# Writing the instruction order of a scan stage and an attention stage by hand on four engines, with side work handed out in small steps

## Chip, cores and metric

The kernel runs on one core of one Trainium2 chip. The metric is the time of one execution in microseconds of device time. Before the change it is 973.29 us, the median of 3 runs (973.04, 973.29, 975.01).

A core has five engines that run side by side, each with its own queue of instructions: PE (TensorE: matrix products and transposes), DVE (VectorE), ACT (ScalarE), POOL (GpSimd) and SP (SyncE, which here only issues transfers). A queue is worked off in order, and an instruction whose input isn't there holds all that stand behind it on its engine. Products land in PSUM, everything else lives in SBUF; DRAM is reached by DMA.

## The reference, cut to what is computed

Four sequences of 512 rows and 128 columns pass through one layer, all in f32:

```python
x = x + A(layernorm(x))        # rmsnorm, selective scan, then mixture of experts
x = x + F(layernorm(x))        # feed-forward, weights are integers / 127
x = x + B(layernorm(x))        # latent attention, 16 heads, causal
x = x + F(layernorm(x))
...
# the scan inside A, 256 channels by 16 states, over 512 rows
h = dA * h + (d_t * x_t)[..., None] * B_t[:, None, :]
y = jnp.einsum('ben,bn->be', h, C_t)
...
# experts inside A: 8 experts, the 2 best of each row
ye = silu(hs @ Wg[e]) * (hs @ Wu[e]) @ Wd[e]
out = out + w_e[:, None] * ye
```

## The kernel before, in words

**Layout.** One sequence is four tiles of 128 rows. `b` counts sequences (0 to 3), `t` row tiles, `e` halves of the 256 channels. Two groups of two sequences share an expert pass: group 0 is sequences 0 and 1, group 1 is 2 and 3.

**Scan stage** (L446 to L758). `front(b)` (L519 to L603) prepares a sequence: normalized rows `hn` and `h0`, transposed (`pt`), convolution products `pm` (L538), `xi`, `sz`, the products for `bc` and `delta`, and `du` (L603, POOL). Then 16 states are scanned one by one, 64 steps in all (`scan(s)`, L635). A step has one chain: PE spreads a row over the partitions (`pb`, L621), DVE multiplies (`bx`, L646), DVE scans (`hst`, L650), POOL multiplies with the row of C (`hc`, L655), PE sums over the states (`yp`, L631). ACT makes the decays of the step two ahead (`da`, L611). `close(b)` (L664) turns `yp` into the output of the scan and the input of the experts, routes every row to two experts (`route`) and gives it a place in a list sorted by expert (`number`). `scatter(b)` writes the rows to the sorted list in DRAM (L268, POOL, 32 indirect transfers in all).

**Experts.** `plan(g)` turns the counts of a group into 23 tiles of 128 rows. `experts(g)` works through them: SP loads the rows `xt` and the weights `wgu` and `wd` (0.83 MB a tile); PE transposes (`mpt`, L353), multiplies (`mpg` and `mpu`, L362, 8 products), ACT takes tanh (L367), DVE two products (`halved`, L323 and L324), PE multiplies (`mpd`, L373), ACT copies (`ym`, L377), SP stores. `combine(b)` gathers the two results of each row (L387, POOL) and adds them (L391, DVE).

**Attention stage** (L761 to the end). `ffn` is a layer norm, a transpose, three pairs of products (`pg` L783, `pu` L785) with tanh and `halved`, and the products `fpd` (L792). `project(b)` makes the latent queries and keys, splits each value into three bf16 parts and stores them in DRAM (`q_d`, `k_d`); `fill(u)` loads them back, stacked, for a unit `u` of 8 heads (8 units). `maxima(u)` finds each row's largest score (`sc`, L886 and L890 on PE, 22 reductions `mx`, L895, on DVE) and sends it through DRAM (`m_d`) into the stack. `exps(G)` makes scores and exponentials of 4 heads (`st` L937 and L945 on PE, `p` L950 on ACT), `weigh(G)` the weighted sums (`po`, L960), `divide(G)` the quotients. 16 of these `G` are run, with `maxima` of the next unit and a queue `work` of side streams between them. Each stream is a Python generator: a `yield` ends one step, and `work.step()` traces the next step of the first stream in the queue.

**What sets the order.** The generators fix only the order in which the program is traced. The order in which each engine gets its instructions is chosen by a scheduler, which goes through what is ready by a priority and an estimated duration; it may put instructions of a side stream before or behind those of the main loop. After the scan stage everything that is left of the queue is emptied (L758), then come `first_ffn(0)`, `project(0)`, the loads of units 0 and 1, and the queue `first_ffn(1), project(1), experts(1), combine(2), first_ffn(2), project(2), combine(3), first_ffn(3)`, 12 steps of it beside `maxima(0)`.

At the start all four sequences are loaded on SP, all their row statistics are taken together in one chain of small DVE instructions on 16 columns (L485 to L496), integer weights are converted (L507) and the two sorted lists are filled with zeros (two transfers of 4 MB, L514).

Of the kernel before, what the change touches and what calls it, by code (L numbers as in the profile page):

```python
# [16 lines left out]
P = 128  # L17
# [9 lines left out]
NG = 4  # L27
EPS = 1e-5
WBUFS = 3
PBUFS = 12  # L30
GROUPS = [[0, 1], [2, 3]]
BIG = 3.0e38


@with_exitstack
def block_kernel(ctx, tc, x, rms1_w, rms2_w, in_proj_w, conv_w, conv_b, x_proj_w,
# [8 lines left out]
    xs = []  # L45
    for b in range(B):
        xt = keep.tile([P, NT, C], F32, tag="x", name=f"x{b}")
        nc.sync.dma_start(xt, x[b].rearrange("(t p) c -> p t c", p=P))
        xs.append(xt)
# [8 lines left out]

    r1w = load("r1w", [P, 1, 1], column(rms1_w, 1), nc.scalar)
    w_in = load("w_in", [P, 2 * EI], in_proj_w, nc.scalar)  # L60
# [4 lines left out]
    A = load("A", [P, NE, NS], A_log.rearrange("(c p) n -> p c n", p=P), nc.scalar)  # L65
    Dk = load("Dk", [P, NE, 1], column(D_skip, NE), nc.scalar)
    w_op = load("w_op", [P, NE, C], out_proj_w.rearrange("(c p) m -> p c m", p=P))
    r2w = load("r2w", [P, 1, 1], column(rms2_w, 1))
    w_rt = load("w_rt", [P, NEXP], router_w)
    w_qk = const.tile([P, 2 * KVL], F32, tag="w_qk", name="w_qk")  # L70
    nc.sync.dma_start(w_qk[:, 0:KVL], W_dqT)
    nc.sync.dma_start(w_qk[:, KVL : 2 * KVL], W_dkvT)
    w_dq = load("w_dq", [KVL, C], W_dq)
    w_uq = load("w_uq", [KVL, C], W_uqT)
    w_uk = load("w_uk", [P, KVL], W_uk)
    w_uv = load("w_uv", [P, KVL], W_uv)
    w_o = load("w_o", [P, C], W_oT)
# [64 lines left out]
    def rsqrt(v, n, pool=small, tag="rs"):  # L142

        r = pool.tile([P, n], F32, tag=f"{tag}{n}", name="rs_r")
        t = pool.tile([P, n], F32, tag=f"{tag}t{n}", name="rs_t")
        nc.vector.tensor_scalar(
            t.bitcast(I32), v.bitcast(I32), 1, None, ALU.logical_shift_right
        )
        nc.vector.tensor_scalar(
            r.bitcast(I32), t.bitcast(I32), -1.0, float(0x5F3759DF), ALU.mult, ALU.add  # L150
        )
        for _ in range(3):
            nc.vector.tensor_tensor(t, r, r, ALU.mult)
            nc.vector.scalar_tensor_tensor(t, t, -0.5, v, ALU.mult, ALU.mult)
            nc.vector.scalar_tensor_tensor(r, t, 1.5, r, ALU.add, ALU.mult)
        return r
# [11 lines left out]
    def layernorm(dst, src):  # L168
        mv = moments(src)
        v = small.tile([P, NT], F32, tag="v", name="ln_v")  # L170
        nc.vector.tensor_scalar(v, mv[:, :, 1], EPS, None, ALU.add)
        r = rsqrt(v, NT)
        for t in range(NT):
            nc.vector.tensor_scalar(
                dst[:, t, :], src[:, t, :], mv[:, t, 0:1], r[:, t : t + 1], ALU.subtract, ALU.mult
            )

# [9 lines left out]
    def transposed(ps, dst, src, scale=None):  # L187

        pt = ps.tile([P, L], F32, tag="mm", name="pt")
# [7 lines left out]
    hs = [keep.tile([P, NT, C], F32, tag="hs", name=f"hs{b}") for b in range(B)]  # L197
# [18 lines left out]
    ps = ctx.enter_context(tc.tile_pool(name="ps_m", bufs=1, space=PSUM))  # L216
# [9 lines left out]
    def number(b):  # L226
# [12 lines left out]
        nc.vector.tensor_copy(tot, pr[:, 1].rearrange("p j e -> p e j"))  # L239
# [14 lines left out]
        nc.vector.tensor_tensor(row, inc.rearrange("p e j -> p j e"), pr[:, 0], ALU.add)  # L254
# [71 lines left out]
    def experts(g):  # L326
# [4 lines left out]
        xT, wgu, wd, hidden = {}, {}, {}, {}  # L331
        for i in range(NTILES + 2):
            if i < NTILES:
                e = nc.sync.value_load(both[0:1, 0, i : i + 1], min_val=0, max_val=NEXP - 1)
                at = nc.sync.value_load(
                    both[0:1, 1, i : i + 1], min_val=0, max_val=NEXP * ROWS - P
                )
                xt = wt.tile([P, C], F32, tag="xt", name="xt", bufs=3)
                nc.sync.dma_start(xt, sorted_x[g][bass.ds(at, P), :])
# [3 lines left out]
                wd[i] = wt.tile([P, NFC, C], F32, tag="wd", name="wd", bufs=WBUFS)  # L343
# [3 lines left out]
            if i >= 2:  # L347
                th, pg, pu = hidden.pop(i - 2)
                hT = wt.tile([P, NFC, P], F32, tag="mh", name="mh")
                halved(hT, th, pg, pu)  # L350
            if i < NTILES:
                pt = ps.tile([P, P], F32, tag="mm", name="mpt")
                nc.tensor.transpose(pt, xt, ident)  # L353
                xT[i] = wt.tile([P, P], F32, tag="xTm", name="xTm", bufs=3)
                nc.scalar.activation(xT[i], pt, AF.Copy, scale=r2w[:, 0, :])  # L355
            if 1 <= i <= NTILES:
                x, w = xT.pop(i - 1), wgu.pop(i - 1)
                pgu = []
                for k in range(2):
                    pp = ps_s.tile([P, NFC, P], F32, tag="sc", name=("mpg", "mpu")[k])  # L360
                    for f in range(NFC):
                        nc.tensor.matmul(  # L362
                            pp[:, f, :], w[:, k, f * P : (f + 1) * P], x, start=True, stop=True
                        )
                    pgu.append(pp)
                th = wt.tile([P, NFC, P], F32, tag="thm", name="thm")
                nc.scalar.activation(th, pgu[0], AF.Tanh, scale=0.5)  # L367
                hidden[i - 1] = th, *pgu
            if i >= 2:
# [6 lines left out]
                y = wt.tile([P, C], F32, tag="ym", name="ym")  # L376
                nc.scalar.copy(y, pd)  # L377
                nc.sync.dma_start(sorted_y[g][(i - 2) * P : (i - 1) * P, :], y)
            yield

    def combine(b):

        g = place[b][0]
        for t in range(NT):
            for k in range(2):
# [4 lines left out]
                )  # L390
                nc.vector.scalar_tensor_tensor(  # L391
                    base[b][:, t, :], yk, gates[b][:, t, k : k + 1], base[b][:, t, :],
                    ALU.mult, ALU.add,
                )
                yield

    class Queue:
# [20 lines left out]
    by_head = w_up.rearrange("p (d h) -> p h d", h=NH)  # L418
    nc.vector.tensor_copy(by_head[0:KVL], w_uq.rearrange("p (h d) -> p h d", d=HS))
    pk = ps.tile([P, L], F32, tag="mm", name="pk")  # L420
    nc.tensor.matmul(pk[:, 0:C], w_uq, w_dq, start=True, stop=True)
    m1 = const.tile([P, C], F32, tag="m1", name="m1")
    nc.vector.tensor_copy(m1, pk[:, 0:C])
    pk = ps.tile([P, L], F32, tag="mm", name="pk")
    nc.tensor.matmul(pk[KVL:P, 0:C], w_uk, m1, start=True, stop=True)
    nc.vector.tensor_copy(
        by_head[KVL:P], pk[KVL:P, 0:C].rearrange("p (h d) -> p h d", d=HS)
    )
    pk = ps.tile([P, L], F32, tag="mm", name="pk")
    nc.tensor.matmul(pk[KVL:P, 0:C], w_uv, w_o, start=True, stop=True)  # L430
    veff = const.tile([P, C], F32, tag="veff", name="veff")
    nc.vector.tensor_copy(veff[KVL:P, :], pk[KVL:P, 0:C])

    vs = []
    for i in range(2):


        va = const.tile([P, NT, NH * (HS + 1) + 32], F32, tag=f"va{i}", name=f"va{i}")
        nc.gpsimd.memset(va, 1.0)
        vs.append(va)  # L440


    nc.scalar.activation(A, A, AF.Exp)
    nc.vector.tensor_scalar(A, A, -1.0, None, ALU.mult)
    work = Queue()
    with ExitStack() as first:  # L446
# [11 lines left out]
        cwb = w3.tile([P, EI, KW], F32, tag="hst", name="cwb", bufs=2)  # L458
        nc.scalar.dma_start(cwb, conv_w.rearrange("e o k -> o e k").to_broadcast([P, EI, KW]))
        for k in range(KW):  # L460
            nc.vector.tensor_tensor(w_k[:, k, :], w_in[:, 0:EI], cwb[:, :, k], ALU.mult)


        w_bc = w1.tile([P, NE, 3, 2 * NS], F32, tag="w_bc", name="w_bc")
        nc.vector.tensor_copy(
            w_bc, w_xp[:, :, DTR:].unsqueeze(2).to_broadcast([P, NE, 3, 2 * NS])
        )
        pick32 = w1.tile([96, 2 * NS], F32, tag="pick32", name="pick32")
        nc.vector.tensor_reduce(
            pick32, ident[0:96, 0:96].rearrange("p (g c) -> p c g", g=3), AX.X, ALU.add  # L470
        )
        pick = w1.tile([96, 2 * NS], BF16, tag="pick", name="pick")
        nc.vector.tensor_copy(pick, pick32)
# [12 lines left out]
        for b in range(B):  # L486
            moments(xs[b], mv0[:, b])
        v = w1.tile([P, B * NT], F32, tag="v0", name="v0")
        var = mv0.rearrange("p b t s -> p (b t) s")[:, :, 1]
        nc.vector.tensor_scalar(v, var, EPS, None, ALU.add)  # L490
        r0 = rsqrt(v, B * NT, w1, "ln")
        nc.vector.tensor_tensor(v, r0, r0, ALU.mult)
        nc.vector.tensor_tensor(v, v, var, ALU.mult)
        nc.vector.tensor_scalar(v, v, EPS, None, ALU.add)
        r01 = rsqrt(v, B * NT, w1, "rms")
        nc.vector.tensor_tensor(r01, r01, r0, ALU.mult)  # L496


        def integers(tag, srcs, dsts):
            raw = w1.tile([P, NE, L], F32, tag=tag, name="raw").bitcast(I32)  # L500
            raw = raw.rearrange("p e l -> p (e l)")
            for i, (src, dst) in enumerate(zip(srcs, dsts)):
                part = raw[:, i * HID : (i + 1) * HID]
                if len(dst.shape) == 3:
                    part = part.rearrange("p (c m) -> p c m", c=NHC)
                nc.sync.dma_start(part, src)
                nc.vector.tensor_scalar(dst, part, 1.0 / 127.0, None, ALU.mult)  # L507

        integers("sp_y", (w_gateT, w_upT), (fwg, fwu))
# [616 lines left out]
```

## Time and profile before

| what | before |
|---|---|
| median of 3 runs | 973.29 us |
| profiled execution: time | 975.5 us |
| profiled execution: span | 973.8 us |
| granted TensorE clock, mean | 0.853 |
| PE busy | 747.4 us (77%), 3588 products |
| DVE busy | 625.7 us (64%), 1266 instructions |
| ACT busy, POOL busy | 332.7 us, 272.7 us |
| moved by DMA | 92.69 MB, mean 95 GB/s |

The profile shows one execution. Its time is 2.2 us over the median, and the 1.7 us between time and span lie outside what the engines do. A line of a group reads: line of the kernel, engine, operation, tile written and tiles read, shapes, count; then the time busy and the mean of one in ns; then the engine's idle time ahead of the group and what ended it. "Idle" is only a loss where the engine sets the pace. A row of the table of windows reads: the window, its length, then busy time and count for PE, its weight loads, DVE, ACT and POOL, then the granted PE clock, the share of time that the DMA engines were busy, and GB/s.

### The profile page before, as it was taken

The numbers are of one execution on the slowest core, as the hardware profiler recorded it, in microseconds if no ns is written. First come the engines' busy times: TensorE is split into PE (matmuls) and PEld (weight loads), VectorE is DVE, ScalarE is ACT, GpSimd is POOL, SyncE is SP. The second block draws the span as 40 slices with busy tenths as digits, with TensorE's granted clock in tenths as the row PEclk, the third lists the DMA queues.
The fourth block names the chain that finished last, engine by engine and source line by source line (L and its number), as shares of the span: only waits on it lengthen the run. The fifth ranks groups of instructions, "written<-read, shape, count | busy, mean of one in ns | idle before, by whom it ended". The sixth has DMA issues, their size and how long they took to land.

```text
span 973.8 us, 11231 instructions
## 1 busy us (share of the span) xinstructions
PE 747.4 (77%) x3588; PEld 407.9 (42%) x3588; DVE 625.7 (64%) x1266; ACT 332.7 (34%) x576; POOL 272.7 (28%) x190
## 2 busy tenths in 40 slices
PE   0878567766687976787266899979478999999894
PEld 0322222323234743575123366866333445444342
DVE  6279899789988899744754655542257475655523
ACT  0477322352236422321011044324311454433440
POOL 2046664476456443613620000000320010000000
PEclk9989796887699988989577589989776899989898
DMA  8612121111115752563146063855400342100000
GB/s 255 235 48 73 43 65 54 44 44 54 55 48 173 218 159 81 156 205 103 44 122 162 18 166 88 242 176 158 112 20 30 87 116 63 39 13 14 3 11 11
DMA packets 81084, 92.69 MB, mean 95 GB/s; under 512 B 9441, under 2 KB 56489, under 8 KB 79849
## 3 DMA queue, kind: packets, MB, share of 16 engines
q1 hardware_dynamic: 77105, 86.81, 30.2%
q0 software_dynamic: 2048, 4.20, 1.5%
q10 hardware_dynamic: 1872, 0.97, 0.4%
q8 instruction: 28, 0.46, 0.2%
q14 instruction: 31, 0.25, 0.1%
HBM read 70.71 MB, written 21.17 MB: 94 GB/s over the span
## 4 chain that ended last, share of the span: by engine, by line
PE 46%; DVE 27%; issue 11%; DMA 7%; ACT 5%; POOL 2%; SPq 1%; ACTq 0%; POOLq 0%; DVEq 0%
DVE hst L650 9%; PE po L960 6%; DVE bx L646 5%; PE yp L631 4%; PE sc L886 4%; PE st L937 4%; PE mpd L373 3%; PE pg L783 3%; DMA xt<-xg 3%; PE mpu L362 3%; PE mpg L362 2%; DVE mx L895 2%; PE fpd L792 2%; DMA yk<-yg,rows_y 2%; PE pm L538 2%
## 5 line engine op out<-in xcount | busy, mean ns | idle before, releaser
L631 PE MATMUL yp<-hc,ident 128*128 128x512 f32 x256 | 165.9, 755 | 69.0 <-POOL hc L655 66.8
L655 POOL TENSOR_TENSOR hc<-hst,cs 128x1024 f32<-128x1024 f32 x64 | 151.2, 2362 | 159.3 <-DVE hst L650 31.4
L650 DVE TENSOR_TENSOR_SCAN hst<-da,bx 128x1024 f32<-128x1024 f32 x64 | 145.9, 2280 | 2.8
L895 DVE TENSOR_REDUCE mx<-sc 128x1 f32<-128x512 f32 (+3 forms) x176 | 109.1, 638 | 43.0 <-PE sc L890 40.8
L611 ACT ACTIVATE da<-delta,A 128x512 f32<-128x512 f32 (+1 forms) x128 | 86.0, 713 | 141.4 <-DVE hst L650 103.1
L950 ACT ACTIVATE p<-st 128x512 f32<-128x512 f32 x160 | 90.9, 597 | 102.7 <-PE st L945 101.3
L631 PEld LDWEIGHTS yp<-hc,ident 128*128 128x128 f32 x256 | 53.6, 229 | 145.3 <-POOL hc L655 109.7
L646 DVE TENSOR_TENSOR bx<-du,pb 128x1024 f32<-128x1024 f32 x64 | 78.5, 1226 | 28.3 <-PE pb L621 24.0
L886 PE MATMUL sc<-ks,qs 72*128 72x128 bf16 (+3 forms) x256 | 71.4, 339 | 9.4 <-DVE mx L895 7.9
L960 PE MATMUL po<-p,va 128*32 128x512 f32 (+3 forms) x512 | 76.3, 447 | 0.0
L323 DVE SCALAR_TENSOR_TENSOR thm<-thm,mpg 128x512 f32<-128x512 f32 x46 | 31.4, 684 | 67.4 <-ACT thm L367 67.4
L387 POOL DMA_INDIRECT yk<-yg,rows_y x32 | 30.4, 950 | 138.5 <-DMA ks<-k_d 128.1
L937 PE MATMUL st<-qs,ks 75*128 75x512 bf16 (+3 forms) x256 | 63.8, 313 | 1.3 <-ACT p L950 0.9
L373 PE MATMUL mpd<-wd,mh 128*128 128x128 f32 x368 | 55.0, 296 | 2.7 <-ACT xTm L355 1.9
L362 PE MATMUL mpu<-xTm,wgu 128*128 128x128 f32 x368 | 53.6, 288 | 3.6 <-DVE mh L324 1.9
L373 PEld LDWEIGHTS mpd<-wd,mh 128*128 128x128 f32 x368 | 49.4, 206 | 13.9 <-ACT xTm L355 9.4
L986 POOL TENSOR_TENSOR base<-x,yn 128x512 f32<-128x512 f32 x4 | 5.1, 1267 | 177.4 <-DVE yn L981 177.4
L362 PE MATMUL mpg<-xTm,wgu 128*128 128x128 f32 x368 | 54.1, 290 | 0.6 <-DVE thm L323 0.6
L362 PEld LDWEIGHTS mpg<-xTm,wgu 128*128 128x128 f32 x368 | 50.4, 207 | 4.1 <-DVE thm L323 1.7
L362 PEld LDWEIGHTS mpu<-xTm,wgu 128*128 128x128 f32 x368 | 48.9, 204 | 7.3 <-DVE mh L324 4.5
L890 PE MATMUL sc<-maskq,identb 128*128 128x128 bf16 (+2 forms) x176 | 48.1, 273 | 0.0
L886 PEld LDWEIGHTS <-qs 72*128 72x128 bf16 x256 | 25.6, 109 | 42.0 <-issue 35.4
(229 smaller groups left out, 1079.9 us busy)
## 6 DMA issues: line engine op xcount, KB each, us to landing
cs<-c_d SPq DMA_DIRECT2D x64, 256.0 KB
wgu<-in_Wg_dram SPq DMA_DIRECT2D x46, 256.0 KB
wgu<-in_Wu_dram SPq DMA_DIRECT2D x46, 256.0 KB
wd<-in_Wd_dram SPq DMA_DIRECT2D x46, 256.0 KB
xg<-zero SPq DMA_DIRECT2D x2, 4096.0 KB
k_d<-parts SPq DMA_DIRECT2D x12, 384.0 KB
qs<-q_d SPq DMA_DIRECT2D x24, 192.0 KB
ks<-k_d SPq DMA_DIRECT2D x24, 192.0 KB
```

Of the source, the lines that this page charges most:

```text
L362: nc.tensor.matmul(pp[:, f, :], w[:, k, f * P : (f + 1) * P], x, start=True, stop=True)
L373: nc.tensor.matmul(pd, hT[:, f, :], w[:, f, :], start=(f == 0), stop=(f == NFC - 1))
L611: nc.scalar.activation(da[:, e, e:], delta[b][:, e, e:], AF.Exp, scale=A[:, e, n : n + 1])
L631: nc.tensor.matmul(yps[b][:, e, :], ident, hc[:, e, :], start=(n == 0), stop=(n == NS - 1))
L646: nc.vector.tensor_tensor(bx, du[b], pb.unsqueeze(1).to_broadcast([P, NE, L]), ALU.mult)
L650: nc.vector.tensor_tensor_scan(hst.rearrange("p e l -> p (e l)"), dec.pop(s).rearrange("p e l -> p (e l)"), bx.rearrange("p e l -> p (e l) ...
L655: nc.gpsimd.tensor_tensor(hc, hst, cs.unsqueeze(1).to_broadcast([P, NE, L]), ALU.mult)
L886: nc.tensor.matmul(sc[:, c : c + w], q[0:NP9, h, t * P : w], k[0:NP9, h, 0:w], start=(h == h0), stop=False, skip_group_check=True,)
L895: nc.vector.tensor_reduce(mx[:, t, h0 : h0 + n], sc[:, 0 : n * w].rearrange("p (h k) -> p h k", k=w), AX.X, ALU.max,)
L937: nc.tensor.matmul(pt[:, c : c + L - kt * P], k[0 : NP9 + 3, h0 + j, rows], q[0 : NP9 + 3, h0 + j, kt * P : L], start=(c == 0), stop=False ...
L950: nc.scalar.activation(p, pt, AF.Exp, scale=scale)
L960: nc.tensor.matmul(po[32 * j : 32 * j + 32, kt * P : L], vs[b % 2][:, kt, (4 * g + j) * (HS + 1) : (4 * g + j) * (HS + 1) + 32], got[j][kt ...
```

## The change

Both stages are put under a manual schedule for PE, DVE, ACT and SP: these four get their instructions in the order in which the program is traced. POOL is left to the scheduler, except that the 64 products `hc` keep their place among the POOL instructions of their step (`queued`). To make the traced order one that can be issued, the side streams are cut into smaller steps, and results that were read at once are read one step later:

- **Start:** only sequence 0 is loaded first; statistics are taken for it alone (4 columns); those of 1 to 3 (12 columns), the integer weights, eight zero fills of 1 MB in place of two of 4 MB, and the weight products `prepare()` move into a stream `early()`, one step of it in each scan step.
- **Scan:** `close` starts at state 1 (was 0), `scatter` at 6 with 2 steps a state (was 4, 3), experts at 9 (was 7); the last sequence takes 2 work steps on odd states. The first feed-forwards of sequences 0 and 1 go into the queue behind the combines. `h2`, `lg` and two count rows are copied by ACT and added by POOL or DVE. 3 buffers for `hc` (was 2), 3 for `cs` (was 4), 2 for `wgu` and `xTm` (was 3).
- **Experts:** `xt` is loaded one iteration ahead of the weights, the result of tile i stored one step later (L328 before: 25 steps, now 27). `combine` adds a step after it gathers (5 steps, was 8).
- **Attention:** the split into three parts and the last addition of `ffn` move from DVE to POOL; the stores to `q_d`, `k_d`, and both transfers of `m_d` move from SP's queue to POOL's; `maxima` reduces a score block one step after its products; `divide` is a part of `weigh`, with a copy by ACT. The side streams are handed out by a rate per step: 0.8, 0.7, then 0.4. Group 1's experts, combines, feed-forwards and projections are in that queue.

```diff
+ORDERED = {ENG.PE, ENG.DVE, ENG.Activation, ENG.SP}
...
+        with tc.manual_schedule(engines=ORDERED):
+            moments(xs[0], mv0[:, 0])
+            deviations([0])
...
+                for n in range(NS):
+                    scan(b * NS + n)
+                    if n >= 1:
+                        next(behind, None)
+                    if n == 6 and b:
+                        rows_out.add(scatter(b - 1))
+                    rows_out.step(2)
+                    if n >= 2:
+                        next(ahead, None)
+                    if n == 9 and b and place[b - 1][1] == len(GROUPS[0]) - 1:
+                        g = place[b - 1][0]
+                        work.add(experts(g), *(combine(i) for i in GROUPS[g]))
+                        work.add(*(first_ffn(i) for i in GROUPS[g]))
+                    next(rest, None)
+                    work.step(2 if b == B - 1 and n % 2 else 1)
...
-        for i in range(NTILES + 2):
-            if i < NTILES:
-                e = nc.sync.value_load(both[0:1, 0, i : i + 1], min_val=0, max_val=NEXP - 1)
+        for i in range(-1, NTILES + 3):
+            if i - 3 in ys:
+                nc.sync.dma_start(sorted_y[g][(i - 3) * P : (i - 2) * P, :], ys.pop(i - 3))
+            if i + 1 < NTILES:
+                k = i + 1
...
+                xt[k] = wt.tile([P, C], F32, tag="xt", name="xt", bufs=3)
+                nc.sync.dma_start(xt[k], sorted_x[g][bass.ds(at, P), :])
...
-            nc.vector.tensor_tensor(dst, src, pd, ALU.add)
+        nc.scalar.copy(o, pd)
+        nc.gpsimd.tensor_tensor(dst, src, o, ALU.add)
...
+                nc.scalar.copy(parts[:, 0, :], pq)
+                nc.scalar.copy(full, pq)
+                nc.gpsimd.tensor_tensor(full, full, parts[:, 0, :], ALU.subtract)
+                nc.gpsimd.tensor_copy(parts[:, 1, :], full)
+                nc.gpsimd.tensor_tensor(parts[:, 2, :], full, parts[:, 1, :], ALU.subtract)
+                if half == 0:
+                    nc.gpsimd.dma_start(q_d.rearrange("j d h l -> (d h) j l"), parts)
...
+        with tc.manual_schedule(engines=ORDERED):
+            work.empty()
+            run(project(0), steps(work, 0))
+            fill(0)
+            fill(1)
+            work.add(experts(1), combine(2), first_ffn(2), project(2))
+            work.add(combine(3), first_ffn(3), project(3))
+            run(chain(project(1)), steps(work, 6))
+            run(times(2, maxima(0)), steps(work, 6))
+            rate = {0: 0.8, 1: 0.8, 2: 0.8, 3: 0.7, 4: 0.7}
...
+                for step in range(10):
+                    credit += rate.get(u, 0.4)
+                    while credit >= 1.0:
+                        work.step()
+                        credit -= 1.0
+                    next(ahead, None)
+                    next(weighed, None)
+                    for _ in range(1 + step % 2):
+                        next(more, None)
```

## The prediction

> **What bounds the kernel now.** I read the page first: the engines' totals, the slices, the chain that ended last; then the rows of the windows cut where the stages change; then the chain itself where PE had holes.
>
> ```profile
> span 973.8 us, 11231 instructions
> PE 747.4 (77%) x3588; PEld 407.9 (42%) x3588; DVE 625.7 (64%) x1266; ACT 332.7 (34%) x576; POOL 272.7 (28%) x190
> ...
> PE 46%; DVE 27%; issue 11%; DMA 7%; ACT 5%; POOL 2%; SPq 1%; ACTq 0%; POOLq 0%; DVEq 0%
> ...
> L650 DVE TENSOR_TENSOR_SCAN hst<-da,bx 128x1024 f32<-128x1024 f32 x64 | 145.9, 2280 | 2.8
> ...
> L646 DVE TENSOR_TENSOR bx<-du,pb 128x1024 f32<-128x1024 f32 x64 | 78.5, 1226 | 28.3 <-PE pb L621 24.0
> ```
>
> No engine is full. The scan step has a floor on DVE: 1.226 (L646) and 2.280 (L650) and 0.23 of gaps in an undisturbed step make 3.75 us, times 64 240 us. The stage lasts from the first `bx` at 56.8 to the last `hst` at 445.3, so 388.5: 148 us above its floor, put there by side streams. By the ends of `hst`, sequence 0 lies 10 over, 1 37 over, the steps up to the experts 27, the rest 74. The attention stage is PE's:
>
> ```profile
> 445.00:540.00 95.00, 53.33 (x194) 29.92 (x195) 47.95 (x214) 11.89 (x23) 31.39 (x29) 0.68 0.35 93
> 540.00:595.00 55.00, 49.73 (x294) 28.54 (x294) 35.92 (x64) 16.47 (x32) 2.30 (x2) 0.74 0.34 96
> 595.00:664.00 69.00, 61.16 (x464) 53.74 (x462) 33.51 (x58) 19.58 (x47) 0.00 (x0) 0.93 0.62 181
> 664.00:694.00 30.00, 27.90 (x202) 18.59 (x200) 6.82 (x10) 15.49 (x33) 1.60 (x2) 1.00 0.56 159
> 694.00:757.00 63.00, 40.82 (x161) 19.58 (x161) 37.50 (x128) 6.53 (x12) 15.92 (x17) 0.64 0.16 45
> 757.00:850.00 93.00, 90.16 (x601) 43.91 (x600) 54.67 (x143) 43.61 (x78) 4.85 (x4) 0.97 0.28 68
> 850.00:948.00 98.00, 91.35 (x567) 43.33 (x565) 48.06 (x125) 40.87 (x73) 1.27 (x1) 0.91 0.06 14
> 948.00:974.00 26.00, 12.62 (x53) 6.85 (x45) 10.14 (x35) 2.96 (x5) 1.26 (x1) 0.87 0.03 10
> ```
>
> See the granted clock, last but two: 0.97 where PE is dense, 0.64 to 0.74 where it waits, and there the same product takes longer. From 445 to 540 and 694 to 757 one stream runs alone, each step behind the last (gathers, layer norm, `pg`, tanh, `halved`). From 595 to 664 no exponentials are made at all: experts go alone, 23 tiles in about 125 us with `maxima`, against 2.9 us of PE for a tile (8 products take 0.89 to 0.95 at full clock, three times, and `mpt`). That is the loss the change can reach.
>
> ```profile
> 482.31 1.10 PE pt L191 x4
> 483.50 0.59 ACT xT L193
> 484.14 2.07 PE pg L783 x2
> ...
> 441.11 3.75 DMA xt<-xg
> 445.48 2.36 POOL hc L655
> ```
>
> **The change part by part,** on the span of 973.8.
>
> *Start.* The first `pt` starts at 24.2 behind statistics of four sequences. With one: `x` lands at 4.4; `bn` and its sums 1.3; 27 dependent instructions at 0.21 (L153, 212 ns) 5.6; `hn` 1.5; `w_k` 2.3: about 15. From `pt` to the first `bx` it was 32.7 (mostly `pm` at a low clock, tables, `delta`); I keep it less 1. First `bx` at 47: **minus 10**. Bounds 0 (the constants land late, SP and ACT share 250 GB/s there) and minus 14.
>
> *Scan.* Sequence 0 takes over what left the start: statistics of three sequences 10.5 (24 small instructions and 27 dependent; DVE is the bound, so nothing hides them), weights 1.4: plus 12. The 8 MB of zeros go through SP ahead of the `cs` of later steps; at the 255 GB/s of the first slice they last 33 us over eight steps of 3.75. `cs` is issued two steps ahead: 0 to 8, I take 2. Sequence 1: step 27 took 15.9 us (5.3 of it waiting for `pb` behind `close` on PE), 28 6.2 (2.1 waiting); written order keeps `spread` ahead of the side stream and spreads `route` and `number` over two more steps: minus 8. Rsqrt links that were handed out two a step (steps 20 to 23 at 4.70) now come in one: 12 at 0.21 and one hold of 2.2, near the 3.8 they cost: 0. Steps 33 to 44: 0. Steps 45 to 63 took 145.7 for 71 of floor. There a step with a tile waits for `xt`, 3.75 to 4.4 us, on the chain, and the last three steps, with about four tiles each, 8.95, 17.8 and 18.1. With `xt` one iteration ahead that wait is hidden; a step with one or two tiles is then PE's: 2.1 (`yp` 1.72, `pb` 0.38) and 1.35 times 2.9, 6 to 7 us. Minus 15, bounds minus 25 and 0 (DVE 3.75 and 1.37 a tile; DMA 0.83 MB at 200 GB/s, 4.2 a tile). Together **minus 9**, last `hst` at 47 + 379 = 426.
>
> *Between.* Before, 127 us lie from the last `hst` to the first `st` of `exps(0)` at 572.4. After: `hc` to `number` took 37.6; the copy by ACT and addition by POOL in place of L682 add 2. POOL puts the scatter of sequence 3 ahead of the last gathers of sequence 1, and DVE its additions ahead of the layer norm: `pt` of the first feed-forward at +48 (was +37). Two feed-forwards at 14.6 (482.3 to 496.9), two layer norms at 4 behind each other, `project(0)` 10.2: +95. Splits on POOL 3 times 1.15 (L820, 1153 ns), stores, loads as before 12: +111. SP's loads of units 0 and 1 stand ahead of the experts' `xt`, so the tiles start there. `project(1)` with three tiles to +126, `maxima(0)` with six tiles 30, and the way through `m_d` 12: first `exps` at +168, **plus 41**. Nine or ten of 23 tiles, 41 us by the pace of the old window, are then done that were not.
>
> *Attention.* From `exps(0)` to the end it was 402. After: PE needs for 8 units of two groups 25.5 each (757 to 850: PE 90, less a feed-forward 8.9 and part of a projection, over about three and a half units), less 14 for `maxima(0)`, 190; 13 tiles 38; 5 feed-forwards at 8.9, 45; 2 projections 9: 282. Issue in order adds what no other PE work may pass: 7 layer norms (13 small instructions at 0.2 and 4 at 0.34, 4 us) 28, and `fpd` behind the last `halved`, 7 times 1.4, 10. That makes 320, a PE share of 0.88 (0.93 to 0.97 in the dense windows of before). The tail, the last feed-forward, stays 26. 346: **minus 56**. Bounds: share 0.95, 297 and 26, minus 79; share 0.80, 352 and 26, minus 24. A work step here has one step of other work between its link on ACT or DVE and the product that reads it; if that cover is gone, see the third rival.
>
> *Moved off DVE and SP.* Eight final additions (0.70 on DVE, L796) become a copy of 0.58 and 1.27 on POOL (L986): 1.2 longer in a chain, 8 times, beside other PE work except the last: 1. Splits are 3.5 on POOL beside tiles. A transfer on POOL's queue occupies it about 0.95 us (L387); POOL is free in attention (5 us of 93), so 0, but a store to `q_d` or `m_d` stands behind a gather that waits for its rows: 0 to 3 each for 4 and 8 of them; taken in the 12 above.
>
> *Two rules of the Trainium skill speak against this.* L600 `delta`, with two inputs in SBUF, takes 2817 ns where L646 of the same size takes 1226, and single rsqrt links of 0.2 us show 2.2 beside `hc`. The page "SBUF — State Buffer", section "A bandwidth-pool intuition that's wrong (but worth ruling out)", says that a DVE instruction with two SBUF inputs is shut out while GpSimd reads SBUF. By it every layer norm beside a split or an addition on POOL would lose up to 2.2 us, which 7 times is 15 at most, where the sum has none; `halved` and `mx` have an input in PSUM and would lose none. The page "DMA: Bandwidth & Descriptors", section "SWDGE vs HWDGE vs iDMA", says that GpSimd builds descriptors in software, slower than the hardware of SP's queue. No row here has the same store on both queues; by it the 12 on `m_d` would grow.
>
> **The sum:** 973.8 - 10 - 9 + 41 - 56 = 940 for the span. The median is 973.29 where this span is 973.8, so about 939.
>
> **The rivals.**
>
> *The gain is deeper.* Tiles and feed-forwards fill every hole: share 0.95 (minus 23), steps 45 to 63 by minus 25 (10 more), `exps(0)` at +160: 899. For it speak the windows at 0.97; against it that those were made by a scheduler that could pass a waiting layer norm by.
>
> *It is hidden anyway: the loads set the pace.* The tile's weights have two buffers where they had three, and 0.83 MB at the 181 GB/s of 595 to 664 take 4.6 us. If the 13 tiles after `exps(0)` and the fills (1.2 MB a unit) keep PE waiting 1.7 a tile and the start gives only half, 22 and 5 are lost: 966. The windows at 0.16 to 0.34 DMA speak against it.
>
> *Slower: the order stalls on a round trip.* In order, PE stands at a side step whose link isn't done, and with it `st` and `sc`, which the scheduler would have put ahead. The place is the 89 work steps of the second stage (27 of tiles, 10 of combines, 40 of feed-forwards, 12 of projections). The price is bounded by a whole round trip, `halved` 0.68 and 0.68 and `mx` 0.64 ahead of it in DVE's queue, 2 us: 178; half of it, 0.75 a step, is 67 and gives 1006. It decides from 34 / 89 = 0.38 us a step. For it: the tiles before had 7.6 us of idle PE-side waits on `halved` in all, with a free order. Against: the steps are written with a step of other work between.
>
> **How the numbers follow.** Forecast 915 to 960, 0.52; deeper, under 915, 0.15; hidden, 960 to 971, 0.09; no change 0.02; slower 0.22, of it half under 995. 0.2% is about what a measurement of this kernel can tell from no change. Range 895 to 995: below it 0.07, above it 0.11. Faster 0.76, same 0.02, slower 0.22.
>
> **What would show it.** First `bx` near 47; last `hst` near 426; the last three scan steps under 9 us; `exps(0)` near 594; in the windows behind it a clock of 0.9 or more throughout and experts' products up to the sixth group or so; no window of the old 694 to 757 kind. Wrong it is if PE waits for DVE in hundreds of short holes (third rival), if `mpg` waits for `wgu` (second), or if DVE's `hst` waits for `cs` or `da` held up behind side work.

## The result, and the profile after

The changed kernel is **slower**: 1061.59 us, median of 4 runs, against 973.16 of before in the same comparison; the ratio of the runs is recorded as 1.094 (1.089 to 1.100), and the two medians alone give 1.091. The forecast was 939, the range ended at 995. The profiled execution has a span of 1060.8.

The page after: the totals, the group whose idle time changed most, and the two groups of the scan that were shown of before:

```profile
span 1060.8 us, 11369 instructions
...
PE 717.3 (68%) x3588; PEld 409.5 (39%) x3588; DVE 636.9 (60%) x1242; ACT 364.8 (34%) x641; POOL 324.2 (31%) x250
...
L964 DVE TENSOR_REDUCE mx<-sc 128x1 f32<-128x384 f32 (+3 forms) x168 | 103.6, 636 | 172.3 <-PE sc L972 172.2
...
L723 DVE TENSOR_TENSOR_SCAN hst<-da,bx 128x1024 f32<-128x1024 f32 x64 | 146.4, 2287 | 7.4
...
L719 DVE TENSOR_TENSOR bx<-du,pb 128x1024 f32<-128x1024 f32 x64 | 78.3, 1224 | 7.2 <-PE pb L679 2.5
```

The first of these groups, in before:

```profile
L895 DVE TENSOR_REDUCE mx<-sc 128x1 f32<-128x512 f32 (+3 forms) x176 | 109.1, 638 | 43.0 <-PE sc L890 40.8
```

PE is busy 30 us less than before and the span is 87 us longer: PE stands idle. The scan instructions themselves take what they took, and DVE waits for `pb` 2.5 us in place of 24; that part of the plan worked. I cut both traces, and those of the experiments, at three events: the first `bx`, the last `hst`, the first `st`. The columns below are the moment of the first `bx`, then the three stretches behind it, and the span, all in us.

| kernel | first `bx` | scan | between | attention | span |
|---|---|---|---|---|---|
| before | 56.8 | 388.5 | 127.1 | 401.4 | 973.8 |
| forecast | 47 | 379 | 168 | 346 | 940 |
| after | 45.2 | 410.3 | 182.0 | 423.3 | 1060.8 |
| e1 order in scan alone | 45.8 | 412.5 | 170.0 | 364.1 | 992.4 |
| e2 order in attention alone | 48.1 | 400.0 | 177.6 | 424.0 | 1049.7 |
| e3 no order | 49.1 | 398.3 | 153.6 | 366.8 | 967.8 |
| e9 PE free in attention | 46.7 | 408.2 | 179.2 | 373.6 | 1007.7 |
| e10 DVE free in attention | 45.6 | 407.4 | 185.8 | 383.8 | 1022.6 |
| e12 no order, two edits | 49.4 | 397.0 | 149.6 | 335.0 | 930.9 |

Some windows of after behind the experts (columns as before), and the whole of attention, first in after, then in e1:

```profile
717.00:751.00 34.00, 23.33 (x119) 11.20 (x119) 20.46 (x57) 9.61 (x17) 8.78 (x10) 0.70 0.15 34
751.00:782.00 31.00, 26.16 (x134) 12.62 (x130) 10.92 (x40) 11.46 (x22) 9.84 (x12) 0.67 0.07 21
782.00:817.00 35.00, 21.82 (x118) 9.74 (x110) 18.07 (x52) 9.41 (x17) 6.78 (x7) 0.76 0.27 70
...
875.00:931.00 56.00, 37.40 (x288) 17.59 (x283) 21.80 (x52) 22.47 (x40) 3.84 (x6) 0.85 0.22 49
...
637.50:1060.80 423.30, 314.83 (x2039) 179.17 (x2038) 186.86 (x486) 154.95 (x286) 53.66 (x60) 0.83 0.20 54
```

```profile
628.30:992.40 364.10, 315.73 (x1968) 165.93 (x1967) 173.34 (x466) 151.13 (x283) 53.75 (x60) 0.91 0.22 62
```

In the first four lines the clock is 0.67 to 0.85, with PE busy 62 to 84% of the time; before had 0.97 and 0.91 from 757 to 948. In the last two lines, the attention of after and of e1, PE is busy for the same 315 us (with 71 products more in after, which had done fewer of them ahead of its first `st`); the 59 by which the two stretches differ are idle PE. What PE waited for there is in the view of waits: us in all, how often, and the longest. After:

```profile
PE st L1021 <- DMA qs<-m_d: 24.2, 4, 8.2
PE pt L169 <- DVE xn L396: 19.6, 5, 6.7
PE sc L968 <- DVE mx L964: 17.4, 13, 6.5
PE pt L169 <- DVE axn L396: 8.7, 2, 5.8
PE pyt L1056 <- ACT ayT L1052: 6.5, 14, 1.0
PE pg L414 <- DVE th L304: 5.3, 6, 1.1
```

e1:

```profile
PE st L1021 <- DMA qs<-m_d: 8.5, 4, 3.4
PE pt L169 <- DVE xn L396: 6.7, 1, 6.7
...
PE sc L968 <- DVE mx L964: 2.0, 5, 1.2
...
PE pt L169 <- DVE axn L396: 1.2, 1, 1.2
```

Three waits make 51 of the 59: the maxima's way through DRAM 16, layer norms 20, score products behind reductions 15. What they are worth is tried further down. One place of the third kind in after, first on DVE, then on PE:

```profile
721.14 0.74 DVE L381 SCALAR_TENSOR_TENSOR base<-yk,gates,base 128x128 f32<-128x128 f32 x2 [5.34 <-DMA yk<-yg,rows_y]
721.80 0.68 DVE L964 TENSOR_REDUCE mx<-sc 128x2 f32<-128x512 f32 x1
...
722.54 0.59 PE L968 MATMUL sc<-ks,qs 72*128 72x256 bf16 x2 [5.22 <-DVE mx L964]
```

DVE stands 5.34 at the sum of a gathered row. The reduction behind it could run, since PE finished its score block at 716.7; the next score products wait for that reduction, which frees their buffer, so PE stands 5.22, and `st` and `po` stand behind them. A wait for a DMA has gone through two queues.

### The profile page after: what moved, and what is told of

It reads as the page before. It is cut to its first block, busy times and chain, and to the rows that moved or that the text cites. A ratio compares the mean times of both kernels' runs of the same rounds, so it can differ in the third digit from the quotient of the medians.

```text
span 1060.8 us, 11369 instructions
## 1 busy us (share of the span) xinstructions
PE 717.3 (68%) x3588; PEld 409.5 (39%) x3588; DVE 636.9 (60%) x1242; ACT 364.8 (34%) x641; POOL 324.2 (31%) x250
## 5 line engine op out<-in xcount | busy, mean ns | idle before, releaser
L964 DVE TENSOR_REDUCE mx<-sc 128x1 f32<-128x384 f32 (+3 forms) x168 | 103.6, 636 | 172.3 <-PE sc L972 172.2
L689 PE MATMUL yp<-hc,ident 128*128 128x512 f32 x256 | 147.2, 705 | 24.7 <-POOL hc L728 15.6
L1034 ACT ACTIVATE p<-st 128x512 f32<-128x512 f32 x160 | 94.4, 599 | 103.1 <-PE st L1029 101.6
L1021 PE MATMUL st<-qs,ks 75*128 75x512 bf16 (+3 forms) x256 | 67.2, 328 | 26.9 <-DMA qs<-m_d 24.2
L968 PE MATMUL sc<-ks,qs 72*128 72x128 bf16 (+3 forms) x256 | 65.9, 325 | 20.3 <-DVE mx L964 19.0
L679 PE MATMUL pb<-bc,pick 96*128 96x512 bf16 x64 | 27.9, 436 | 70.9 <-DVE bx L719 69.6
L997 POOL DMA_DIRECT2D m_d<-mT x8 | 4.4, 554 | 210.8 <-ACT mT L995 210.8
L1046 PE MATMUL po<-p,va 128*32 128x128 f32 (+3 forms) x512 | 53.0, 492 | 0.0
L360 PE MATMUL mpd<-wd,mh 128*128 128x128 f32 x368 | 51.9, 287 | 0.1
L354 ACT ACTIVATE thm<-mpg 128x512 f32<-128x512 f32 x46 | 27.5, 597 | 50.3 <-PE mpg L348 49.7
```

The costliest lines, as they stand in the source:

```text
L360: nc.tensor.matmul(pd, hT[:, f, :], w[:, f, :], start=(f == 0), stop=(f == NFC - 1))
L689: nc.tensor.matmul(yps[b][:, e, :], ident, hc[:, e, :], start=(n == 0), stop=(n == NS - 1))
L964: nc.vector.tensor_reduce(*taken, AX.X, ALU.max)
L968: nc.tensor.matmul(sc[:, c : c + w], q[0:NP9, h, t * P : w], k[0:NP9, h, 0:w], start=(h == h0), stop=False, skip_group_check=True,)
L1021: nc.tensor.matmul(pt[:, c : c + L - kt * P], k[0 : NP9 + 3, h0 + j, rows], q[0 : NP9 + 3, h0 + j, kt * P : L], start=(c == 0), stop=False ...
L1034: nc.scalar.activation(p, pt, AF.Exp, scale=scale)
```

## The experiments

**Which order costs.** In e1 the manual schedule around attention is taken away, in e2 the two of the scan stage, in e3 all three; e4 is the kernel before with its two stages put under the order for the same four engines, and nothing else.

```diff
-        with tc.manual_schedule(engines=ORDERED):
+        with ExitStack():
```

> The changed kernel with the manual order kept in the scan stage alone; the attention stage is left to the scheduler. Theory A (the written order itself costs: an instruction that waits holds the engine): the 28 us that PE waited for layer norms, the 17 for sums behind gathers and part of the low clock behind 717 come back, 990 to 1020. Theory B (the order is free, what costs is how the steps were cut, delayed and moved to other queues): 1050 to 1065, as with the order.

> The changed kernel with the manual order kept in the attention stage alone; the scan stage is left to the scheduler. Theory A: the scan stage, 410 us from the first bx to the last hst with the order, falls to 385 or less, 1025 to 1040. Theory B: 1050 to 1065.

> The changed kernel without any manual order: all its steps, moves and loads, order by the scheduler. Theory A: the sum of both parts comes back, 950 to 985, so at or below the kernel before. Theory B: over 1040.

> The kernel before with the two stages under the manual order and nothing else changed: its steps read results at once that the changed kernel reads a step later. Theory A: 60 us or more slower than before, 1035 to 1150. Theory B: within 20 us of 973.

Measured: e1 989.72, 1.016 (1.005 to 1.027); e2 1047.81, 1.076 (1.067 to 1.084); e3 968.92, 0.993 (0.986 to 0.999); e4 1211.64, 1.244 (1.231 to 1.256). e1, e3 and e4 fall to theory A, e4 beyond what I gave it; e2 lies between the two theories, 14 under the changed kernel: the scan stage has the smaller part. Of the 25 us by which e1's span exceeds e3's, 14 lie in the scan and 16 between, less 3 at the start and 3 in attention. The order costs 93 us on the changed steps (1061.6 against 968.9) and 237 on the steps of before. So the change's other edits, cutting and delaying the steps among them, were worth much under the order, and not enough; which of them, e4 doesn't separate.

**Which wait.** Three edits in the changed kernel, order kept, and e8 with all three. e5 moves the layer norm's `yield` from behind `moments` to behind the last `tensor_scalar`; e6 lets `combine` of group 1 add two steps after the gather (6 buffers `yk`); e7:

```diff
-                    for _ in range(1 + step % 2):
+                    for _ in range(2):
                         next(more, None)
```

> Order kept in both stages; the layer norms' step boundary is moved from behind the moments to behind the normalized rows, so that PE's transpose is issued one step later and the number of steps stays. In the trace of the changed kernel PE waits 28 us for layer norms behind exps(0), against 8 with the scheduler. Theory C (the 58 us that order costs in attention are PE's waits at products of side streams, each at its own place): these 20 go, 1040. Theory D (the hold only moves to the next product in the queue, because DVE is late anyway, or the clock eats it): under 5, 1056 to 1062.

> Order kept; the combines of group 1 add their gathered rows two steps after the gathers instead of one, with 6 buffers for the rows (was 4). PE waits 17 us for mx behind exps(0), 2 with the scheduler, because mx stands behind these additions on DVE. Theory C: 12 to 15 less, 1047. Theory D: under 5.

> Order kept; maxima gets two steps in each of the 20 steps of a unit instead of one and two in turn, so that it ends about 7 steps ahead of the exponentials that need it and the way through m_d is covered. PE waits 24 us for qs from m_d, 8 with the scheduler. Theory C: 16 less, 1045. Theory D, or DVE's reductions become what is waited for: under 5, 1056 or more.

> The three edits together, order kept. Theory C: they add up, 50 less, 1010, which is still 20 over the 990 of order in the scan stage alone. Theory D: 1050 or more.

Measured: e5 1059.67, 1.095 (1.090 to 1.100); e6 1051.00, 1.086 (1.082 to 1.089); e7 1044.34, 1.078 (1.072 to 1.083); e8 1034.03, 1.069 (1.065 to 1.073). Against 1.094 that is 0, 8, 16 and 25 us: theory C for e7, theory D for e5, and e8 is about the sum of e6 and e7, half of the 50 expected. In e7 the wait it aimed at is 24.2 no more:

```profile
PE st L1021 <- DMA qs<-m_d: 6.0, 1, 6.0
```

e6 gets half to two thirds of what theory C gave it, but its interval touches that of the changed kernel, and the wait it aimed at hardly moved: `sc` for `mx` is 15.3, from 17.4. In e5 PE's waits at `pt` fall from 28.3 to 22.1 and those of `sc` for `mx` rise from 17.4 to 21.5: the norm's chain of 5 us lies on DVE in one piece, and I take it that whoever needs DVE next pays. In e1 the scheduler laid the links of two norms (757 to 762 and 801 to 808) between reductions.

**Which engine's order.** e9 leaves PE out of the set in attention, e10 DVE.

```diff
-        with tc.manual_schedule(engines=ORDERED):
+        with tc.manual_schedule(engines=ORDERED - {ENG.PE}):
```

> Scan stage ordered as in the changed kernel; in the attention stage the order holds for DVE, ACT and SP, and PE is left to the scheduler. Theory E (PE's own order is what costs: a product of a side stream that waits holds the scores behind it): most of the 72 us between the changed kernel and order in the scan stage alone come back, 995 to 1015. Theory F (DVE's order costs: layer-norm chains and sums stand ahead of the reductions that PE's score products wait for; the other engines only show it): 1045 to 1062.

> The same with the order for PE, ACT and SP, and DVE left to the scheduler. Theory E: 1045 to 1062. Theory F: 995 to 1015. If neither gives back more than 20, the two orders hold each other and only both free help.

Measured: e9 1011.67, 1.039 (1.031 to 1.046); e10 1027.57, 1.055 (1.046 to 1.064). PE free gives back 50 of the 72 us between after and e1, DVE free 34. e9 lies in the range of theory E, e10 in neither; the two gains sum to more than 72, so they overlap. In e10 the waits for `mx` fall to 6.7 while those for `qs` stay (21.2): a free DVE didn't help PE past a load. In e9 those for `qs` fall to 4.3.

**The second projection, and no order with better steps.** e11 traces `project(1)` ahead of the experts:

```diff
+            run(project(1))
             work.add(experts(1), combine(2), first_ffn(2), project(2))
             work.add(combine(3), first_ffn(3), project(3))
-            run(chain(project(1)), steps(work, 6))
-            run(times(2, maxima(0)), steps(work, 6))
+            run(times(2, maxima(0)), steps(work, 12))
```

e12 is e3 with the edits of e7 and e11; e13 is e3 with e7's alone, e14 with e11's alone, e15 is e1 with both.

> Order kept everywhere; project(1) is traced as a whole ahead of the first step of the experts, and maxima(0) gets the six steps that stood beside it. In the changed kernel PE stood 20.5 us at the first mpt, waiting for xt, with the second projection's products and the first scores behind it. If that wait held work that was ready, exps(0) comes 10 to 20 earlier and the end with it, 1042 to 1052. If the loads of the units and xt are late anyway, under 5.

> No order at all, with project(1) first and maxima at two steps: what the two edits that helped or may help under the order give without it. The scheduler already passes a waiting product by, so 960 to 970, as without the edits; if the maxima's way through m_d is late there too (PE waits 8 us for it), up to 8 less.

> No order; maxima at two steps alone. In the trace without order PE waits 10.8 us for qs from m_d and 8.9 in front of st for nothing shown; with both edits neither is in the list. If the maxima are the cause: 940 to 950, most of the 34 us. If not: 965 to 970.

> No order; project(1) first alone. Under the order it gave 12 us. Without it the scheduler passes the waiting xt by: 960 to 970 if the maxima are the cause of the 34, 940 to 950 if it is this.

> Order in the scan stage alone, both edits in attention. The order's price in the scan stage was 21 us by e1 against e3 (989.7 and 968.9), 14 by the changed kernel against e2. If it is a price of that stage, 953 to 958; if it was slack that attention took up, within 5 of 935.

> The version without order, with project(1) first and maxima at two steps, as in the run of 934.9: a ratio of 0.955 to 0.970 to before.

Measured: e11 1048.41, 1.076 (1.069 to 1.084); e12 934.94, 0.960 (0.953 to 0.967); again as e18 932.81, **0.963 (0.958 to 0.967)**; e13 938.82, 0.969 (0.961 to 0.977); e14 960.50, 0.993 (0.990 to 0.996); e15 952.19, 0.981 (0.973 to 0.989). e11 as expected. For e12 my expectation was wrong by 30: I took the scheduler to make the rate of `maxima` indifferent. It doesn't. In e3 the maxima of unit 1 end late, and its first `st` starts at 680.1; in e12 it starts at 659.1, and that of unit 7 at 876.9 in place of 913.4. Maxima are the source of every unit, and a step rate that was too low held all units behind it, with the order (e7) and without it (e13). e12 beats both kernels. e15, whose four runs spread from 943 to 958, says that the price of the order in the scan stage stays when attention is better: 18 us by the ratios, give or take 9.

A part of the attention of e18, to be read beside before's windows of 0.64 and of 0.97:

```profile
690.00:740.00 50.00, 46.58 (x217) 23.35 (x218) 30.04 (x93) 20.24 (x37) 15.06 (x17) 0.78 0.14 46
740.00:800.00 60.00, 59.78 (x388) 29.45 (x386) 39.24 (x119) 29.83 (x54) 14.39 (x16) 1.00 0.35 86
```

**The moved queue.** e16 is e12, e17 the changed kernel, with these back on SP:

```diff
-            nc.gpsimd.dma_start(m_d.rearrange("i h l -> (i h) l"), mT)
-            nc.gpsimd.dma_start(q[NP9 : NP9 + 3, :, :], m_d)
+            nc.sync.dma_start(m_d.rearrange("i h l -> (i h) l"), mT)
+            nc.sync.dma_start(q[NP9 : NP9 + 3, :, :], m_d)
...
```

> No order, both edits, and the stores to q_d, k_d and the transfers of m_d put back from POOL's queue to SP's, as before the change. If POOL's queue is a part of the loss, 922 to 930. If SP's loads hold them up there, or POOL was free anyway, 933 to 945.

> The changed kernel, order kept, with the stores to q_d and k_d and both transfers of m_d on SP's queue again. If POOL's queue is a part of the loss (the way through m_d made PE wait 24 us): a ratio to before of 1.075 or less. If SP, whose order is now written too, holds them behind loads that wait for buffers: 1.10 or more. If it doesn't matter: 1.085 to 1.10, as the changed kernel's 1.094.

Measured: e16 942.03, 0.975 (0.969 to 0.981); e17 1039.75, 1.074 (1.068 to 1.080). Under the order the move to POOL is 20 us of the loss; without it the move gains 12 (0.963 of e18 against 0.975, both to before). The wait of e17:

```profile
PE st L1021 <- DMA qs<-m_d: 7.3, 4, 2.8
```

It is 24.2 in after. In both kernels `st` waits for this way in units 0, 4, 5 and 7. From the end of ACT's copy `mT` to that `st` it takes 8.6, 8.6, 9.7 and 5.2 us in after, and 3.6, 3.6, 4.3 and 3.6 in e17. Unit 7 is the last and has no loads beside it: there the way is 1.6 us longer on POOL's queue. In the other three, one of POOL's two transfers landed 5.4 to 6.5 us after its issue, where the medians of all eight units are

```profile
m_d<-mT POOLq DMA_DIRECT2D x8, 24.0 KB, 1.7
qs<-m_d POOLq DMA_DIRECT2D x8, 24.0 KB, 2.5
```

While these three were out, about 1 MB of SP's loads moved and the DMA engines were busy 0.61 to 0.75 of the time (0.75 in unit 4, 882.3 to 888.4), against 0.03 beside the transfer of unit 7. In e17 SP issues both transfers ahead of the loads of the next unit. So most of the longer way goes with the loads that the transfers met on POOL's queue, and less with that queue itself; no run holds the loads back alone. e7 and e17 take away the same wait by two ways, and were not tried together.

In e16 the way is covered, and SP's own queue stands at the store for `mT`, with loads behind it:

```profile
SPq L997 <- ACT mT L995: 114.6, 6, 27.1
```

That this is why e16 is slower is read from the trace, not tried.

## Why the prediction was wrong, step by step

**Start:** minus 10 was forecast, minus 11.6 measured.

**Scan:** minus 9 was forecast, plus 22 measured. I count steps from 0, and from the first `bx` to the ends of `hst` of steps 16, 32, 44 and 63. Sequence 0 (to step 16): plus 14 forecast (12, and 2 for `cs`), plus 18 measured. I said that nothing hides the statistics; what the order takes away is their cover. DVE in the stretch ahead of the first `bx`, e3 and after:

```profile
16.00:31.00 15.00, 14.13 (x28) 5.59 (x27) 7.54 (x45) 4.76 (x8) 0.00 (x0) 1.00 0.00 0
```

```profile
16.00:31.00 15.00, 14.92 (x30) 5.59 (x30) 0.30 (x3) 5.12 (x9) 0.00 (x0) 1.00 0.00 0
```

The scheduler puts 45 DVE instructions into PE's convolution, the order leaves DVE with 3. From the first `bx` to the first of sequence 1, e3 then takes 66.0 and after 88.2, while the first `bx` of e3 comes 3.9 later. Sequence 1 (17 to 32): minus 8 forecast, minus 2 measured; steps 33 to 44: 0 forecast, plus 11, and as much in e3, so it comes from the new steps and not from the order (which of them was not tried). Steps 45 to 63: minus 15 forecast, minus 5. Behind sequence 0 the order is ahead of the scheduler: sequence 1 takes 94.4 in after and 101.7 in e3, steps 45 to 63 take 140.9 and 144.0. What the order costs between the first `bx` and the last `hst`, 12 us, lies in sequence 0 alone. With two tiles in a step DVE stands at the second, ahead of the next `bx`:

```profile
344.75 0.69 DVE L304 SCALAR_TENSOR_TENSOR thm<-thm,mpg 128x512 f32<-128x512 f32 x1 [4.05 <-ACT thm L354]
345.54 0.69 DVE L305 SCALAR_TENSOR_TENSOR mh<-thm,mpu 128x512 f32<-128x512 f32 x1
346.15 1.22 DVE L719 TENSOR_TENSOR bx<-du,pb 128x1024 f32<-128x1024 f32 x1
```

Most steps with one tile take 4.90 (three take 7.1 to 10.4), those with two 9.3 to 11.8 (17.7 beside a layer norm of `close`), where I gave 6 to 7 for either.

**Between:** plus 41 was forecast, plus 55 measured. The chain was right to its middle: first `pt` at +46 (forecast +48), the first tile at +116 (+111). At that tile PE had stood 20.5 for its rows `xt`, with the second projection ready behind it; e11, with that projection first, makes this stretch 17.9 shorter. Another 6.5 were for `m_d`.

**Attention:** minus 56 was forecast, plus 22 measured; this is the step that failed. "Issue in order adds what no other PE work may pass" had two terms, 7 layer norms at 28 and `fpd` at 10. The layer norms were 28.3, to the point, and `fpd` 2.1. But I asked only which side-stream products would wait, and not which products of the main loop would: `st` for `m_d` 24, `sc` for `mx` 17, `pyt` for `ayT` and `pg` for `th` 12 were in no term. The second of them is two queues deep. For the move to POOL's queue I wrote "POOL is free in attention (5 us of 93), so 0"; e17 makes it 20. I had asked whether POOL was busy, and not which loads its transfers would meet.

Of the 77 us over the forecast's 346, 57 are idle PE (108 against 38 and some 13 in the tail). The other 20 are PE busy longer, 315 against 282 and 13; one tile more than the 13 I gave was left, and the clock was 0.83 where e12 below has 0.93; what each is worth was not tried. The forecast's 346 was reached, and passed, by e12 with 335, without the order:

```profile
591.00:931.00 340.00, 298.21 (x1994) 163.29 (x1994) 178.98 (x477) 150.66 (x284) 53.70 (x60) 0.93 0.27 73
```

With 298 busy there, the floor of PE work was sound; its cover under the order was not.

**The rivals.** The slower one came, and went past the 1006 that it gave. Its price was 0.75 us on each of 89 steps; the 77 us over the forecast in attention make 0.87. Its picture was not right, so the nearness of the two prices is luck: not hundreds of short holds but some forty behind `exps(0)`, eleven of which (at `st` for `m_d` and at `pt`) make 52 of the 82 us listed above. "Against: the steps are written with a step of other work between" was the error: a step of the main loop is about 2 us of PE (315 us over 160 steps), and the links to cover are 5 (a layer norm on DVE), 5.3 (what was left of a gather) and 5.2 to 9.7 (through DRAM). The rival in which the loads set the pace did not come: `mpg` waited 2.7 us for `wgu` in attention.

**POOL's queue, and POOL beside DVE.** The Trainium skill, "DMA: Bandwidth & Descriptors", section "SWDGE vs HWDGE vs iDMA", has descriptors built in software for a transfer from GpSimd's queue, with a faster setup from SP's. The row that bears on it is unit 7, 5.2 us on POOL's queue against 3.6 on SP's: right in direction, and small beside the 20 of e17. The prediction's other rule, on DVE instructions with two inputs in SBUF, stands in "SBUF — State Buffer" under "Who interferes with whom", and not in the section that the prediction names. A row of after agrees: one link of a norm that starts with an addition on POOL takes 1.26, where its neighbours take 0.16. What all such holds cost was not added up.

```profile
516.38 1.25 POOL L429 TENSOR_TENSOR x<-base,fo 128x512 f32<-128x512 f32 x1 [14.21 <-DVE rs_t L142]
...
516.21 0.16 DVE L142 SCALAR_TENSOR_TENSOR rs_t<-rs_t,ln_v 128x4 f32<-128x4 f32 x1
516.40 1.26 DVE L143 SCALAR_TENSOR_TENSOR rs_r<-rs_t,rs_r 128x4 f32<-128x4 f32 x1
```

## What to carry to other kernels

When an order is written by hand, price each wait for every instruction behind it on that engine, and follow it into the next queue: a late input of a side stream can cost the main loop its full length, as the gather did at 721. Distance in steps is worth what the steps last: compare it with the link's own latency, the longest (a DMA round trip) first. When a transfer moves to another queue, ask which loads it will no longer be ahead of. And look at what the scheduler put into holes before replacing it; here the same new steps without the order, with the second projection first and the maxima issued sooner, were 4% faster than before.

## What the runs showed that I had not expected

One queue's move had both signs: it cost 20 us under the order and gained 12 without it. And the rate at which a source stream is traced (maxima at 1.5 or 2 steps) was worth 16 us under the order and 23 to 32 without it (0.969 of e13 against 0.993 of e3, 0.960 of e12 against 0.993 of e14), though the scheduler was free to reorder.
